# Latent cross-attention of a two-layer decoder: the context's keys and values between the first projections, the second batch's rows among the first batch's scores

## The chip, the core and the metric

The kernel runs as one program on one core of a Trainium2 chip. The metric is the device time of one execution in microseconds. The engines are named as the profile names them: PE does the matmuls and the transposes (PEld is its weight load), DVE, ACT and POOL do elementwise work and reductions, SP issues the DMAs. Each engine works through its own queue in order; an instruction waits for the semaphores of the engines whose results it needs.

## What is computed

The program is a decoder of two layers on `x` of shape 4 x 1024 x 256 (four batches, 1024 rows, 256 features), float32, with a context of 4 x 77 x 256. Layer 0 is causal attention, cross-attention and a quantised feed-forward; layer 1 is an attention with a convolution over the heads, the latent cross-attention, and a mixture of experts. The change touches the latent cross-attention and what is prepared for it inside the layer-1 attention. Its reference, cut to what matters (`x` is the context here, `latents` are the normalised rows of the decoder):

```python
xn = layernorm(x, ln_x_g, ln_x_b)            # 77 context rows of a batch
ln = layernorm(latents, ln_l_g, ln_l_b)      # 1024 rows of a batch
q = ln @ W_q
kv = concat([xn @ W_kv, ln @ W_kv], axis=1)  # 77 + 1024 keys and values
k, v = kv[..., :256], kv[..., 256:]          # then 4 heads of 64
qn = rmsnorm(q, q_gamma) * 64 ** -0.5
kn = rmsnorm(k, k_gamma)
sim = where(full_mask, qn @ kn.T, neg)       # the mask hides context rows only
out = softmax(sim) @ v @ W_out + b_out       # added to x of the decoder
```

## The kernel before, in words

**The stage.** `Latents.run` (L1874) does the latent cross-attention, batch after batch. Its PSUM has two rotating slots named `pt` for projections and transposes (`ps_t`, `bufs=2`), one set of score tiles, one of outputs. A tile of a name takes the next slot of that name and waits until the one before in that slot has been read. The order of PE, ACT and DVE is the order in which the Python code records the instructions (`manual_schedule`), so generators that are advanced by `next` decide what stands between what.

**The pieces of the work.**
- `of_context` (L1911) makes the context's keys and values. For each of the four batches it projects 77 rows (L1919, two matmuls 512 wide), copies the keys out and squares them on ACT (L1922, L1924), copies the values on DVE (L1925) and sums the squares (L1926). Then come the inverse root mean squares of all four (L1900 and the steps L86 to L94), the scaling of the keys (L1907), and for each batch two transposes (L1935) whose results two DVE instructions copy into `kcT` with the factor gamma (L1938). In the kernel before this runs as one block, and its keys stand in a tile `k`.
- `projected(b)` (L1942) does the same for the 1024 rows of a batch, in eight tiles of 128 rows: key and value projection (L1956), query projection (L1958), four ACT instructions (L1960, L1961, L1963, L1964), the value copy on DVE (L1962) and the sum of squares (L1965). Then the inverse roots (L1900, L86 to L94, L1976), scaling of the keys in two halves (L1907) and transposes of queries and keys in groups of four (L1983) which ACT copies out (L1984). It yields after each tile, and five times in the rest: 13 steps.
- `rows(b)` (L1815) normalises the rows of a batch of `x`: statistics in two halves on DVE (L1823, L1824), inverse roots (L101, L86 to L94), normalisation in two halves of four DVE instructions (L118), and for each half two groups of four transposes (L1838) that two ACT instructions each copy out (L1811).
- `ahead(b, got)` (L2122) advances `projected(b)` and, from its tenth step on, `rows(b + 1)`: 16 steps.
- The unit: for a batch, for four pairs of row blocks, two head pairs and two blocks there are 16 units. In each, the scores are computed on PE (L2008, L2012, L2016), their maxima on DVE (L2021, L2023, L2024), exponentials on ACT (L2035, L2041), the probabilities of the unit before are transposed (L2058, L2065) and copied (L2059, L2066), and the values are weighed (L2090). Each unit advances the next batch's preparation, `coming = ahead(b + 1, got)`, by one step.
- `add_row` (L156) adds the output's bias to a whole batch of `x` on POOL. `projected(b)` calls it after its first tile, and it waits until `rows(b)` has read `x`.

**The order at the start of the stage.** The small constants are prepared (L2136 to L2147), then `of_context()` runs as a block, then all 16 steps of `ahead(0)`, that is the projections of batch 0 with the rows of batch 1 in the last steps, and only then the first unit.

**What runs earlier.** The layer-1 attention `l1_attn` takes a generator `beside` (defined in `network`) that it advances once in four scores, 16 times in the last batch, and to the end when its own work is over. It yields from `latents.context` (normalises and transposes the context, L1864) and `latents.rows(0)`. There `pt` has a single slot. In `rows` of the kernel before, the two groups of transposes of a half stand in one step; the second group needs the slot of the first. The attention's own chain per score is PE L1520, DVE L1528, POOL L1530, DVE L1538, ACT L1541, and PE weighs the values of four scores together (L1549).

## Time and profile before

| what | value |
|---|---|
| median of 3 runs | 4223.02 us (4222.13 to 4224.56) |
| the profiled execution, own time | 4222.46 us |
| its span | 4220.7 us |
| PE busy | 3950.9 us, 94% of the span |
| DVE busy | 2984.2 us, 71% |
| ACT busy | 1622.8 us, 38% |
| POOL busy | 1019.4 us, 24% |
| mean granted clock of PE | 0.973 |
| first context projection (L1919) starts | 2892.03 us |
| first projection of batch 0 (L1956) starts | 2911.48 us |
| first scores (L2008) of batch 0, 1, 2, 3 start | 2956.86, 3118.65, 3293.51, 3462.52 us |

The profile tells the times of one execution, counted from the start of its span. A timeline row gives start, duration, engine, line, what is written from what, and behind it the idle time ahead of it with the engine that ended it. PE's clock can be granted in full or in part; the profile gives its mean for a stretch.

### The profile page before, as it was taken

The page shows a single profiled execution, that of the slowest core. Times are in us where ns is not written, and L with a number is a line of the kernel's source. Part 1 is how long each engine was busy: PE and PEld are TensorE (multiplying, and loading weights), DVE is VectorE, ACT ScalarE, POOL GpSimd, SP SyncE. Part 2 cuts the span into 40 slices and gives each one's busy share as a digit, 9 for nine tenths or more (in the row PEclk, how much of TensorE's full clock was granted, in tenths as well). Part 3 has the DMA queues.
Part 4 walks back from the last instruction along what each step waited for, and adds up shares of the span by engine and source line. Part 5 has one row for each costly group of instructions (what it writes and reads, how often), then busy time and mean ns, then how long its engine had stood idle before and what let it go on. Part 6 is the DMA issues. An engine that isn't in the chain of part 4 may idle for free.

```text
span 4220.7 us, 58215 instructions
## 1 busy us (share of the span) xinstructions
PE 3950.9 (94%) x22392; PEld 2841.7 (67%) x22392; DVE 2984.2 (71%) x5514; ACT 1622.8 (38%) x2601; POOL 1019.4 (24%) x1218
## 2 busy tenths in 40 slices
PE   8899568999999999999999999997989899899999
PEld 6644335887788887888878877784555555557765
DVE  6646688888878888788878889776566567543324
ACT  4334355334333343333433333332555454212221
POOL 1100000433333433334333343331000000012215
PEclk9989889999999999999999999998999999899999
DMA  2010000000000000000000000000000000302213
GB/s 68 2 40 1 1 23 1 1 1 1 1 1 1 1 1 1 1 1 1 1 1 1 1 1 1 1 1 27 1 1 1 1 1 11 114 23 62 63 43 109
DMA packets 50911, 64.37 MB, mean 15 GB/s; under 512 B 8557, under 2 KB 44769, under 8 KB 50625
## 3 DMA queue, kind: packets, MB, share of 16 engines
q1 hardware_dynamic: 44145, 42.81, 3.2%
q0 software_dynamic: 6480, 17.70, 1.5%
q8 instruction: 185, 3.03, 0.3%
q14 instruction: 101, 0.83, 0.1%
HBM read 42.80 MB, written 17.69 MB: 14 GB/s over the span
## 4 chain that ended last, share of the span: by engine, by line
PE 67%; DVE 15%; ACT 1%; issue 1%; DMA 0%; SPq 0%; DVEq 0%; ACTq 0%
PE sc L1520 35%; PE po L1549 5%; PE ph L2572 4%; PE ph L2500 3%; PE sc L2008 3%; DVE mx L1528 3%; DVE pr L1538 3%; DVE nm L2021 3%; PE po L2090 2%; PE po L2602 2%; PE po L2487 2%; PE pt L1956 2%; DVE prT L2059 1%; DVE km L1510 1%; PE pt L2058 1%
## 5 line engine op out<-in xcount | busy, mean ns | idle before, releaser
L1520 PE MATMUL sc<-qT,km 128*128 128x256 f32 x8064 | 1793.1, 381 | 8.8 <-DVE pr L1538 8.8
L1520 PEld LDWEIGHTS sc<-qT,km 128*128 128x128 f32 x8064 | 1521.4, 190 | 273.7 <-issue 61.4
L1541 ACT ACTIVATE pr<-pr,zb 128x1024 f32<-128x1024 f32 x512 | 588.2, 1149 | 1326.3 <-DVE pr L1538 1298.5
L1530 POOL PARTITION_ALL_REDUCE top<-mx x512 | 544.6, 1064 | 1465.6 <-DVE mx L1528 1465.6
L1528 DVE TENSOR_REDUCE mx<-sc 128x256 f32<-128x1024 f32 x512 | 625.4, 1221 | 321.3 <-PE sc L1520 320.0
L1538 DVE TENSOR_TENSOR pr<-sc,top 128x1024 f32<-128x1024 f32 x512 | 621.0, 1213 | 0.0
L1510 DVE SCALAR_TENSOR_TENSOR km<-kT,w_L_attn_conv_w,km 128x512 f32<-128x512 f32 x504 | 380.3, 757 | 25.2 <-ACT km L1497 20.4
L1533 POOL COPY tops<-top 32x256 f32<-32x256 f32 x512 | 269.9, 527 | 32.6
L1549 PE MATMUL po<-pr,v 128*32 128x256 f32 x4096 | 248.4, 383 | 0.0
L2021 DVE TENSOR_REDUCE nm<-sc 128x1 f32<-128x1024 f32 x128 | 156.1, 1220 | 77.3 <-PE sc L2008 77.2
L2035 ACT ACTIVATE pr<-sc,nb,rq 128x1024 f32<-128x1024 f32 x128 | 155.0, 1211 | 128.0 <-PE pt L2065 110.6
L1549 PEld LDWEIGHTS po<-pr,v 128*32 128x32 f32 x4096 | 120.3, 110 | 109.3 <-issue 42.7
L2572 PE MATMUL ph<-wgu,xnT 128*128 x568 | 179.8, 459 | 0.6 <-ACT xnT L2561 0.6
L1497 ACT ACTIVATE km<-kT,w_L_attn_conv_w 128x512 f32<-128x512 f32 x252 | 173.5, 706 | 5.3 <-PE po L1303 5.3
L2579 DVE TENSOR_TENSOR xnT<-ph,xnT 128x352 f32<-128x352 f32 x71 | 37.2, 524 | 187.7 <-ACT xnT L2578 187.7
L2058 PE MATMUL pt<-ident,pr 128*128 128x128 f32 x1024 | 142.9, 280 | 22.2 <-DVE X L2109 12.8
L2073 POOL COPY rb<-rinv 128x256 f32<-128x256 f32 x32 | 12.8, 400 | 591.4 <-DVE rinv L2049 313.9
L2058 PEld LDWEIGHTS pt<-ident,pr 128*128 128x128 f32 x1024 | 111.6, 142 | 47.3 <-issue 18.8
L2090 PE MATMUL po<-prT,v 128*64 128x256 f32 x1024 | 133.5, 393 | 0.2 <-DVE oT L2097 0.2
L2572 PEld LDWEIGHTS ph<-wgu,xnT 128*128 128x128 f32 x568 | 102.3, 190 | 46.0 <-ACT xnT L2561 0.9
L2008 PE MATMUL sc<-kT,qT 64*128 64x512 f32 x512 | 130.8, 615 | 0.3 <-ACT pr L2035 0.3
L2059 ACT COPY prT<-pt 128x512 f32<-128x512 f32 x128 | 68.9, 588 | 142.3 <-PE pt L2058 142.3
(518 smaller groups left out, 4882.6 us busy)
## 6 DMA issues: line engine op xcount, KB each, us to landing
yrows<-xnT SPq DMA_DIRECT2D x71, 128.0 KB, 1.7
X<-in_x SPq DMA_DIRECT2D x8, 512.0 KB, 7.3
out<-X SPq DMA_DIRECT2D x8, 512.0 KB, 3.1
wgu<-in_L_ffn_w_gate SPq DMA_DIRECT2D x8, 352.0 KB, 6.4
wgu<-in_L_ffn_w_up SPq DMA_DIRECT2D x8, 352.0 KB
raw<-in_L_ffn_w1T SPq DMA_DIRECT2D x4, 512.0 KB, 3.5
raw<-in_L_ffn_w2T SPq DMA_DIRECT2D x4, 512.0 KB, 3.6
xrows<-xn SPq DMA_DIRECT2D x2, 1024.0 KB, 4.5
```

Of the source, the lines that this page charges most:

```text
L1510: nc.vector.scalar_tensor_tensor(km, keys, weight, km, ALU.mult, ALU.add)
L1520: nc.tensor.matmul(sc[:, j, :], km[:, c, bass.ts(j, P)], qT[:, c, bass.ts(i, Q2)], start=(c == 0), stop=(c == 1),)
L1528: nc.vector.tensor_reduce(mx, sc.rearrange("p j q -> p q j"), AX.X, ALU.max)
L1530: nc.gpsimd.partition_all_reduce(top, mx, P, bass_isa.ReduceOp.max)
L1533: nc.gpsimd.tensor_copy(tops[n][rows, i % (NQ, 2)[n], :], top[rows])
L1538: nc.vector.tensor_tensor(pr, sc, top.unsqueeze(1).to_broadcast([P, KT, Q2]), ALU.subtract)
L1541: nc.scalar.activation(pr, pr, AF.Exp, bias=zb[:, h : h + 1])
L1549: nc.tensor.matmul(po[32 * e : 32 * e + 32, :], v[:, n * KT + j, 4 * g + e, :], prs[e][:, j, :], start=(j == 0), stop=(j == KT - 1),)
L2008: nc.tensor.matmul(sc[e][:, bass.ts(n, 512)], lhsT[at], kT[at, d, bass.ts(n, 512)], start=True, stop=True,)
L2021: nc.vector.tensor_reduce(nm, sc[e], AX.X, ALU.max, negate=True)
L2058: nc.tensor.transpose(pt[:, n, :], pr[e][:, bass.ts(j + n, P)], net.ident)
L2572: nc.tensor.matmul(ph[:, k, :F], s["xT"][:, c, :], wgu[:, bass.ds(s["e"] * GU + (2 * c + k) * F, F)], start=(c == 0), stop=(c == 1),)
```

## The change

The change has three parts. No arithmetic is added or left out.

1. `of_context` becomes a generator of ten steps; its keys stand in a buffer of `v` instead of `k`, and the copy with gamma into `kcT` goes from DVE to ACT. At the start of the stage four of its steps alternate with the first four tiles of `projected(0)`; the small constants come after these, and the rest of the context stands between the later steps of `projected(0)`.
2. `rows(1)` is no longer done ahead of the first scores. `ahead(1)` does it first, in three steps, within the first three units of batch 0, and squeezes `projected(1)` and `rows(2)` into the other 13.
3. `rows(0)`, beside the layer-1 attention, gets `fine=True`: a yield after each group of four transposes.

```diff
-    def rows(self, b, ps):
+    def rows(self, b, ps, fine=False):
...
                     self.lg, self.lb,
                 )
+                if fine:
+                    yield
...
             def of_context():
-                kc = p1.tile([P, NTB, D], F32, name="k")[:Z, :B]
+                kc = p2.tile([P, NTB, D], F32, name="v")[:Z, :B]
...
                         sums[:, b, :], sq.rearrange("p (h d) -> p h d", h=H), AX.X, ALU.add
                     )
+                    yield
                 flat = sums.rearrange("p b h -> p (b h)")
                 r = inverse_rms(flat, Z, B * H, "rc").rearrange("p (b h) -> p b h", h=H)
+                yield
                 times_rms(kc, r, Z)
+                yield
...
-                        nc.vector.tensor_scalar(
-                            kcT[at, :, b, e, :], pt[at, :2, :Z], gk[at], None, ALU.mult
+                        nc.scalar.activation(
+                            kcT[at, :, b, e, :], pt[at, :2, :Z], AF.Copy, scale=gk[at]
                         )
+                    yield
...
             def ahead(b, got):
+                if b == 1:
+                    for k, _ in enumerate(self.rows(b, ps_t)):
+                        if k % 2:
+                            yield
+                    yield
                 now, rows = projected(b, got), self.rows(b + 1, ps_t) if b + 1 < B else iter(())
-                for k in range(16):
+                for k in range(16 if b > 1 else 13):
                     next(now, None)
-                    if k >= NTB + 1:
+                    if b == 1 and k == 12:
+                        next(now, None)
+                    for _ in range((k >= NTB + 1) + (b == 1 and k > 10)):
                         next(rows, None)
                     yield
...
+                kcT = w.tile([P, 2, B, 2, Z], F32, name="kcT")
+                nc.gpsimd.memset(kcT, 0.0)
+                vc = w.tile([P, B, D], F32, name="vc")
+                got = []
+                now, context = projected(0, got), of_context()
+                for _ in range(4):
+                    next(context)
+                    next(now)
                 nc.vector.tensor_scalar(gq, gq, float(dh) ** -0.5, None, ALU.mult)
...
-                of_context()
-                got = []
-                for _ in ahead(0, got):
+                for k in range(12):
+                    next(now, None)
+                    if k in (0, 2, 5, 6, 7, 8):
+                        next(context, None)
+                for _ in chain(context, now):
                     pass
...
-                        yield from latents.rows(0, ps)
+                        yield from latents.rows(0, ps, fine=True)
```

More of the change, by code (lines that the diff above doesn't have):

```diff
@@ L2144, in run @@
                 nc.vector.memset(first[0:1], 1.0)
-                kcT = w.tile([P, 2, B, 2, Z], F32, name="kcT")
-                nc.gpsimd.memset(kcT, 0.0)
-                vc = w.tile([P, B, D], F32, name="vc")
-                of_context()
-                got = []
-                for _ in ahead(0, got):
+                for k in range(12):
[3 more added lines that the diff above has]
+                for _ in chain(context, now):
                     pass
```

## The prediction

> **What bounds the kernel now.** I read first the busy time by stretches of the latent stage (length, then busy time and instructions of PE, PEld, DVE, ACT, POOL, then PE's granted clock, DMA share, GB/s), with a second cut for the clock:

> ```profile
> 2892.00:2911.50 19.50, 9.07 (x25) 3.38 (x25) 12.45 (x34) 2.69 (x8) 5.33 (x2) 0.85 0.48 146
> 2911.50:2940.00 28.50, 25.96 (x72) 13.25 (x72) 9.57 (x19) 11.01 (x33) 0.00 (x0) 0.92 0.00 1
> 2940.00:2957.00 17.00, 9.13 (x42) 7.08 (x44) 13.71 (x53) 7.61 (x14) 2.07 (x1) 0.60 0.00 0
> 2957.00:3118.70 161.70, 146.25 (x854) 85.57 (x854) 106.49 (x243) 88.60 (x208) 9.77 (x9) 0.98 0.00 1
> ```
> ```profile
> 2943.00:2957.00 14.00, 7.89 (x34) 6.24 (x36) 11.09 (x40) 5.55 (x10) 2.07 (x1) 0.51 0.00 0
> 2957.00:2962.00 5.00, 5.00 (x20) 2.36 (x20) 3.02 (x5) 2.35 (x5) 2.45 (x1) 1.00 0.00 0
> ```

> The context's block (row 1) and the stretch between the last projection and the first scores (row 3) are bound by DVE's chain, with PE half idle; the projections (row 2) and batch 0's units (row 4) fill PE. Then the timeline names the waits:

> ```profile
> 2900.20 4.48 POOL L156 TENSOR_TENSOR X<-X,r_L_xattn_b_out 128x2048 f32<-128x2048 f32 x1 [7.35 <-issue]
> ...
> 2901.66 3.05 DVE L1900 TENSOR_SCALAR ss_c<-ss_c 77x16 f32<-77x16 f32 x1
> ...
> 2908.37 0.75 PE L1935 MATMUL pt<-ident,k 77*128 77x77 f32 x4 [8.21 <-DVE k L1907]
> ...
> 2918.30 1.03 PE L1958 MATMUL pt<-w_L_xattn_W_q,xnT 128*128 128x256 f32 x4
> ...
> 2919.68 1.98 PE L1956 MATMUL pt<-w_L_xattn_W_kv,xnT 128*128 128x512 f32 x4 [0.34 <-DVE v L1962]
> ...
> 2952.73 1.98 PE L1838 MATMUL pt<-ident,xn 128*128 128x128 f32 x8 [3.14 <-DVE xn L118]
> ```

> PE stands 8.21 us for the context's roots, and 3.14 us for batch 1's normalisation, which the first scores do not need. In the layer-1 attention the same view shows PE waiting for ACT at the second group of four transposes of `rows(0)`, twice:

> ```profile
> 2637.23 1.12 PE L1838 MATMUL pt<-ident,xn 128*128 128x128 f32 x4 [4.29 <-ACT xnT L1811]
> ...
> 2660.26 1.11 PE L1838 MATMUL pt<-ident,xn 128*128 128x128 f32 x4 [3.44 <-ACT xnT L1811]
> ```

> **Part 1: context between the projections.** A tile runs from key projection to key projection in 3.20 us (2916.48 to 2919.68): 1.82 until PE starts the query (2918.30), then ACT's two readings, DVE's value copy and the slot. A context projection has the same four records as the key projection, so 1.82 more per piece, if the slots allow. They do: the query's slot is freed by the context's value copy, which ends about 3.14 after the piece's start (2.03 to ACT's first reading as from 2916.48 to 2918.51, 0.66 for both, 0.45 for DVE), and PE wants it at 3.64. Four pieces: 4 x 5.02 = 20.1 us. Wq's DMA starts at 2891.66 and lands in 2.7 us, ahead of the first use at 2895.7.

> Then four tiles, 4 x 3.20 = 12.8. DVE must do beside them the constants (0.15, 0.32, 0.31, 0.11, 0.17: 1.06), the context's roots (2.45: rows 2904.75 to 2907.01 and 0.20 for L1900 unblocked, as at 2939.93) and the scaling (1.22). Between its sum and the next value copy it is idle 1.64; the constants and the scaling fit, the roots are late by 0.8. From the last tile's end to its sum's end 1.1 (2938.83 to 2939.90). Sum: the last sum is ready 20.1 + 12.8 + 0.8 + 1.1 = 34.8 after the first context matmul; before, 2939.90 - 2892.03 = 47.9. POOL's addition, which held L1900 for 3.05 us, meets only value copies and sums there, and L1925 and L1926 ran at 0.42 and 0.40 inside it. If the constants and the scaling found no idle DVE, they would add 2.3. No DMA is moved, and POOL keeps its order here: the zeroing of `kcT`, then the addition. The keys' new buffer is one of the two of `v`: batch 1's values take it long after its last reading, and batch 2's wait for batch 0's last weighing, as now (DVE idles 11.61 us before L1962 at 3137.52).

> **Part 2a: rows(1) taken from ahead of the scores.** From that sum to the first scores now: 2956.86 - 2939.90 = 17.0. After: 4.5 to the first key transposes, unchanged (2944.41). DVE's second scaling follows the first at once, without the four statistics pairs between (2.05). Then two rounds of eight key transposes with two context groups between and behind, by ACT's copies: four at 0.69 and four of the `kcT` form. That form is not shown on ACT; the copy of 77 x 256 starts its successor 0.26 later, L2059's 512 columns take 0.59; I take 0.37, DVE's present time. With transposes at half clock (1.94 per eight, as now) the scores start 9.7 after the sum, at full clock 8.4; I take 9.1. First scores at 34.8 + 9.1 = 43.9, before 64.8: **-20.9 us**.

> **Part 2b: rows(1) in the first three units.** Batch 0 takes 161.8 us now (first scores 2956.86 to 3118.65). Starts of the scores give the costs: units without preparation, from the last batch, 8.60, 9.50, 7.75, 8.22; units with a tile, from unit 3 of batch 0, 10.84, 11.38, 12.08, 10.52.
> - Units 0 to 2: now 28.2. Unit 0's maxima end at 4.9; eight statistics pairs (4.24) push the next maximum to 9.2, where it is at 9.03 now, as a tile's copy and sum stood there. In unit 1, roots (2.4) and half the normalisation (1.36) follow DVE's last copy at 13.9: next maximum 17.8, now 20.05, as the tile at half clock (3.62) is gone. In unit 2 come 16 transposes through two slots, each group waiting for two ACT copies (0.96) behind unit 2's exponentials: scores 3 at 27.0. Gain 1.2, with no tile done.
> - Units 3 to 10: eight tiles, 55.7 as now for the first five and 34.0 for three that have other work now: 89.6.
> - Unit 11 roots 8.3. Units 12, 13 query transposes with half the statistics each, 9.8 and 10.7 (now 10.67, 9.25 on other base units). Unit 14 key transposes with roots and normalisation: DVE 9.9, I take 10.0. Unit 15 key transposes (1.0) and all 16 row transposes: four waits for 0.96 us of ACT behind the exponentials, 8.2 + 1.0 + 4.0 = 13.2.
> Sum 27.0 + 89.6 + 8.3 + 9.8 + 10.7 + 10.0 + 13.2 = 168.6 against 161.8: **+6.8 us**.

> POOL's addition for batch 1 moves from 2954.93 to the end of unit 2's normalisation. Queued behind it are the copies `rb`, needed two units on. It can stop DVE:

> ```profile
> 3099.39 4.53 POOL L156 TENSOR_TENSOR X<-X,r_L_xattn_b_out 128x2048 f32<-128x2048 f32 x1 [15.10 <-DVE xn L118]
> ...
> 3102.16 1.78 DVE L2024 SCALAR_TENSOR_TENSOR nb<-nm,nx,rq 128x1 f32<-128x1 f32 x1
> ```

> L2024 takes 0.22 elsewhere and here ends when POOL does: 1.56 lost. In unit 2 POOL would run from 24.3 to 28.8 and the next L2024 stand at 30.5, so I count nothing; the bounds are 0 and 1.56. [...]

> **Part 3: four transposes at a time.** From one weighing of values (L1549) to the next takes 15.88 us where nothing stands beside. With the first normalisation it took 18.35 (2612.07 to 2630.42), with group, wait, group and second normalisation 23.89, with group, wait, group 21.77: 8.01 + 5.89 = 13.90 extra. After: four intervals with one group each and one with the normalisation (2.47). A group costs between 0.26 (the four context transposes at 2533.7: 16.14) and its own 1.12 at half clock; I take 0.6: 2.47 + 4 x 0.6 = 4.9. **-9.0 us**, between -11 and -7. The cover is the slot: its copies must be done 14 us later, where 4.29 was enough now.

> **Sum.** -20.9 + 6.8 - 9.0 = -23.1, so 4222.46 - 23.1 = 4199.4 for the profiled execution. The median of the runs lies 0.56 above it: **4200.0 us**.

> **Rivals.**
> - *Half clock in the first units* (0.16). With the tiles gone from units 0 to 2, PE idles for DVE and ACT; now 2943 to 2957 stood at 0.51, and the clock rose just when the scores began. If all three units' scores (2.7 each on the path, with sx and mask) run at half clock: 3 x 2.7 = 8.1, 4208.1. For it: the idle times in units 0 and 1; against: scores follow densely packed projections. [...]
> - *The rows come due in batch 0* (0.12): rows(2), squeezed into units 14 and 15, makes DVE and ACT the bound and adds its DVE time again (statistics apart: 2.4 + 2.7 + 1.2) and 4 more of waits: +10.3, 4210.3.
> - *fine changes nothing* (0.08): the group waits for a slot at another place, since there is only one. Without part 3: 4209.0.
> - *Slower* (0.03): PE's half clock lasts through the tile units of batch 0. A unit has some 10.5 us of PE work, so each unit at half clock adds up to that; 2.2 such units eat the 23.1 us, and with four the time is 4199.4 + 0.6 + 42 = 4242. Against it: in batch 0 the clock is 0.98, as tiles and scores keep PE filled.

> **How the numbers follow.** The forecast has 0.61. Its own bounds: part 1 and 2a +-2, 2b +-4, part 3 +-2, so 4193 to 4207. The range reaches up to the rivals at 4208 to 4210 and leaves some 0.13 out: 4193 to 4211. Differences within 0.2% (8.4 us, about what a measurement of this kernel can tell from none) need 14.7 us of the gain lost: two rivals together, 0.04 of their 0.36. Faster 0.93, slower 0.03.

> **What would show it.** First scores 44 us after the first context matmul; the pieces every 5.0 us; no L1900 of 3 us; intervals of L1549 with single groups near 16.5; batch 0 near 168.6 between first scores. The forecast is wrong if a piece takes 6 or more (a slot wait I missed), if the clock row of the first 20 us of batch 0 is near 0.5, or if unit 15 takes over 17.

## The result, and the profile after

The changed kernel takes **4195.34 us** (median of 4 runs, 4194.45 to 4199.97), the kernel before on the same chip 4222.58 us (4 runs, 4219.43 to 4224.56): ratio 0.9941, 95% interval 0.9925 to 0.9956 (the quotient of the two medians, 0.9935, lies inside it). A later comparison (run e9 below) gave 0.9941 again (0.9927 to 0.9954). The prediction was 4200.0 us, range 4193 to 4211, faster with 0.93: the direction is right, the range holds the time, and the forecast is 4.7 us too slow.

The profiled execution has a span of 4192.5 us, before 4220.7. Here is where the 28.2 us between them lie, from the starts of the groups of records in both traces (line numbers of the changed kernel, where the scores are L2014, the context projections L1921):

| stretch | before, us | after, us | difference | predicted |
|---|---|---|---|---|
| start to the weighing of values (L1549) at 2496.33 / 2488.91 | 2496.33 | 2488.91 | -7.4 | 0 |
| from there to the last L1549 (`rows(0)` beside) | 386.86 | 374.63 | **-12.2** | -9.0 |
| from there to the first context matmul | 8.84 | 8.81 | 0.0 | 0 |
| first context matmul to first scores | 64.83 | 43.28 | **-21.6** | -20.9 |
| batch 0, first scores to first scores | 161.79 | 171.91 | **+10.1** | +6.8 |
| batches 1, 2 and 3 | 474.62 | 475.89 | +1.3 | 0 |
| last scores to the end | 627.41 | 629.07 | +1.7 | 0 |

The first row has nothing to do with the change: no instruction differs there. The same weighing stands at 2490.91, 2493.92, 2498.69, 2497.40, 2495.68, 2492.03 and 2491.14 in the profiled executions of e1 to e6 and e9, whose instructions up to there are all the same. What differs is PE's clock: up to 2488 us it was granted in half for 112.6 us in this execution and for 136.5 us in the one of before, and over the fourteen profiled executions the weighing tends to start later the longer that time is (from 2488.91 us with 112.6 to 2498.92 us with 146.8, in e7). So one pair of profiles can be up to 10 us apart before the edit begins, and the change itself is worth -20.8 us by the rows behind the first.

The windows that answer to the ones of before (length, then busy time and instructions of PE, PEld, DVE, ACT, POOL, then PE's granted clock, DMA share, GB/s); the rows are the projections with the context, the way from the last sum to the first scores, units 0 to 2, and the rest of batch 0:

```profile
2872.00:2906.00 34.00, 30.49 (x88) 14.71 (x88) 15.98 (x44) 13.46 (x41) 5.63 (x2) 1.00 0.29 84
2906.00:2915.60 9.60, 6.79 (x33) 4.95 (x32) 5.15 (x17) 6.69 (x14) 0.00 (x0) 0.69 0.00 0
2915.60:2946.60 31.00, 24.93 (x97) 12.89 (x96) 21.34 (x62) 15.81 (x37) 4.04 (x2) 0.76 0.00 1
2946.60:3087.50 140.90, 128.89 (x774) 76.20 (x772) 92.35 (x218) 76.17 (x179) 7.06 (x8) 1.00 0.00 1
```

The block of 19.5 us with PE half idle is gone: context and projections are one stretch of 34 us, 90% PE, at full clock. The poor stretches are now the second and the third, at a clock of 0.69 and 0.76. The timeline of PE shows both (start, duration, engine, line, out<-in, count, idle time ahead and what ended it):

```profile
2872.35 1.94 PE L1921 MATMUL pt<-w_L_xattn_W_kv,cT 128*77 128x512 f32 x4 [0.52 <-DVE X L1608]
2874.13 1.88 PE L1962 MATMUL pt<-w_L_xattn_W_kv,xnT 128*128 128x512 f32 x4
2875.85 1.03 PE L1964 MATMUL pt<-w_L_xattn_W_q,xnT 128*128 128x256 f32 x4
2877.22 1.94 PE L1921 MATMUL pt<-w_L_xattn_W_kv,cT 128*77 128x512 f32 x4 [0.34 <-DVE v L1968]
...
2908.43 0.35 PE L1940 MATMUL pt<-ident,v 77*128 77x77 f32 x2
2910.57 1.94 PE L1989 MATMUL pt<-ident,k 128*128 128x128 f32 x8 [1.79 <-DVE k L1909]
...
2915.63 3.79 PE L2014 MATMUL sc<-kT,qT 64*128 64x512 f32 x8
2919.35 0.81 PE L2018 MATMUL sx<-kcT,qT 128*128 128x154 f32 x2
2920.00 0.23 PE L2022 MATMUL sx<-mrow,first 128*128 128x77 bf16 x2
2922.60 5.17 PE L2014 MATMUL sc<-kT,qT 64*128 64x512 f32 x8 [2.36 <-ACT pr L2041]
...
2946.65 1.99 PE L2014 MATMUL sc<-kT,qT 64*128 64x512 f32 x8
```

A piece (L1921 to the next L1921) takes 4.87 us and its projections wait only 0.34 for a slot. Eight score matmuls take 1.99 us in unit 3; in unit 0 they take 3.79 and in unit 1 5.17, which includes a wait for ACT inside the group.

In the attention, the waits of 4.29 and 3.44 us ahead of the second group are gone: a weighing of values (L1549), then one group of 0.66 us, no wait, and the next weighing 16.27 us after the last.

```profile
2623.03 1.93 PE L1549 MATMUL po<-pr,v 128*32 128x256 f32 x32
2624.89 0.66 PE L1838 MATMUL pt<-ident,xn 128*128 128x128 f32 x4
...
2639.30 1.93 PE L1549 MATMUL po<-pr,v 128*32 128x256 f32 x32
2641.16 0.66 PE L1838 MATMUL pt<-ident,xn 128*128 128x128 f32 x4
...
2655.56 1.93 PE L1549 MATMUL po<-pr,v 128*32 128x256 f32 x32
...
2671.52 1.93 PE L1549 MATMUL po<-pr,v 128*32 128x256 f32 x32
```

### The profile page after: what moved, and what is told of

Read it like the earlier page. It is cut to its first block, busy times and chain, and to the rows that moved or that the text cites. A ratio compares the mean times of both kernels' runs of the same rounds, so it can differ in the third digit from the quotient of the medians.

```text
span 4192.5 us, 58206 instructions
## 1 busy us (share of the span) xinstructions
PE 3941.7 (94%) x22392; PEld 2833.7 (68%) x22392; DVE 2978.4 (71%) x5506; ACT 1626.6 (39%) x2609; POOL 1019.4 (24%) x1218
## 4 chain that ended last, share of the span: by engine, by line
PE 68%; DVE 15%; ACT 1%; issue 1%; DVEq 0%; ACTq 0%
PE sc L1520 35%; PE po L1549 5%; PE ph L2594 4%; PE ph L2522 3%; PE sc L2014 3%; DVE mx L1528 3%; DVE nm L2027 3%; DVE pr L1538 3%; PE po L2096 2%; PE po L2624 2%; PE po L2509 2%; PE pt L1962 1%; DVE prT L2065 1%; DVE km L1510 1%; PE pt L2064 1%
## 5 line engine op out<-in xcount | busy, mean ns | idle before, releaser
L1528 DVE TENSOR_REDUCE mx<-sc 128x256 f32<-128x1024 f32 x512 | 625.7, 1222 | 308.5 <-PE sc L1520 307.3
L1549 PE MATMUL po<-pr,v 128*32 128x256 f32 x4096 | 248.4, 383 | 0.0
L1549 PEld LDWEIGHTS po<-pr,v 128*32 128x32 f32 x4096 | 120.2, 110 | 109.3 <-issue 42.7
L2079 POOL COPY rb<-rinv 128x256 f32<-128x256 f32 x32 | 12.8, 400 | 632.0 <-DVE rinv L2055 389.9
L2014 PE MATMUL sc<-kT,qT 64*128 64x512 f32 x512 | 136.0, 629 | 2.6 <-ACT pr L2041 2.4
```

Source lines behind the costliest of these rows:

```text
L1528: nc.vector.tensor_reduce(mx, sc.rearrange("p j q -> p q j"), AX.X, ALU.max)
L1549: nc.tensor.matmul(po[32 * e : 32 * e + 32, :], v[:, n * KT + j, 4 * g + e, :], prs[e][:, j, :], start=(j == 0), stop=(j == KT - 1),)
L2014: nc.tensor.matmul(sc[e][:, bass.ts(n, 512)], lhsT[at], kT[at, d, bass.ts(n, 512)], start=True, stop=True,)
```

## The experiments

All runs are compared with runs of the kernel before on the same chip; e1 to e4 shared one chip, e5 to e8 a second, e9 to e11 a third, and e12 ran on a fourth. Since the total moves by several us without an edit, most verdicts below rest on the intervals of the trace. "Front" is first context matmul to first scores; "batch 0" is first scores of batch 0 to first scores of batch 1, and so on.

| run | time, us | ratio (95%) | front | units 0-2 | batch 0 | batch 1 | batch 2 |
|---|---|---|---|---|---|---|---|
| before, profiled | 4222.46 | | 64.8 | 28.2 | 161.8 | 174.9 | 169.0 |
| after, profiled | 4194.45 | | 43.3 | 31.0 | 171.9 | 175.6 | 169.5 |
| e1 part 3 alone | 4206.66 | 0.9968 (0.9956-0.9980) | 65.1 | 28.4 | 161.9 | 175.3 | 169.1 |
| e2 part 1 alone | 4204.21 | 0.9960 (0.9947-0.9974) | 50.75 | 28.4 | 162.0 | 175.0 | 169.0 |
| e3 part 2 alone | 4217.58 | 0.9992 (0.9983-1.0001) | 56.3 | 28.5 | 169.4 | 175.4 | 169.2 |
| e4 added matmuls | 4192.05 | 0.9927 (0.9912-0.9942) | 41.9 | 26.8 | 167.6 | 172.4 | 169.4 |
| e5 parts 1 and 3 | 4201.69 | 0.9949 (0.9936-0.9963) | 50.75 | 29.0 | 160.9 | 172.9 | 169.5 |
| e6 later tiles | 4196.98 | 0.9937 (0.9922-0.9952) | 43.1 | 29.8 | 170.7 | 169.6 | 165.3 |
| e7 e4 and e6 | 4192.36 | 0.9926 (0.9912-0.9939) | 41.9 | 26.8 | 167.6 | 170.3 | 165.3 |
| e8 shifted normalisation | 4201.59, one run | | 42.7 | 29.9 | 170.8 | 175.4 | 169.2 |
| e9 changed kernel again | 4195.36 | 0.9941 (0.9927-0.9954) | 43.1 | 29.9 | 170.75 | 175.0 | 169.3 |
| e10 e4 and e8 | 4191.20 | 0.9926 (0.9913-0.9940) | 41.9 | 26.8 | 167.65 | 172.4 | 169.2 |
| e11 e4, e6 and e8 | 4186.93 | 0.9917 (0.9903-0.9930) | 41.9 | 26.8 | 167.65 | 170.4 | 165.1 |
| e12 added transposes | 4198.62, one run | | 41.9 | 28.7 | 169.6 | 173.0 | 169.7 |

**e1: part 3 alone.** The kernel before with `fine`:

```diff
-                        yield from latents.rows(0, ps)
+                        yield from latents.rows(0, ps, fine=True)
```

> The kernel before with the single transpose groups of rows(0) alone (part 3). Theory: the part stands by itself. From the first weighing of values (L1547 or so, as the lines stand) behind rows(0)'s start to the last one, the extra over 15.88 us a piece falls from 13.90 to about 1.6 us, as in the changed kernel: 12.2 us, so 4210.4 against 4222.6, and all behind it in the latent stage as before (front 64.8 us from the first context matmul to the first scores, batch 0 161.8 us). Rival (drift): the 12.2 us were partly a luck of the clock windows in one profiled execution; then the extra is 5 us or so here, as predicted (-9.0), and the time is 4213 to 4214. A step of the clock windows ahead of the attention, where the instructions are the same, may move the profiled times by several us either way: that the 7.4 us by which the changed kernel was early there are of this kind is shown if this kernel's own first weighings stand elsewhere too.

Measured: from the same weighing to the last one 374.61 us, before 386.86: -12.25, and 13.5 by the ratio (0.0032 x 4222). The part stands by itself and everything behind is as before. The rival falls.

**e2: part 1 alone.** The changed kernel's start of the stage, with the old `ahead`, with `rows(0)` as before (no `fine`), and with

```diff
+                rows = self.rows(1, ps_t)
                 for k in range(12):
                     next(now, None)
                     if k in (0, 2, 5, 6, 7, 8):
                         next(context, None)
+                    if k > 4:
+                        next(rows, None)
-                for _ in chain(context, now):
+                for _ in chain(context, now, rows):
```

> The context's keys and values between the first batch's projections (part 1), with rows(1) left ahead of the first scores and rows(0) as before. Theory: the last sum is ready 33.7 us after the first context matmul (before 47.9, changed kernel 33.7): -14.2; from there to the first scores 17.0 as before plus some 1.5 for the keys' transposes that now stand there: first scores at 52.2 instead of 64.8, -12.6; batch 0 161.8 as before. Time 4222.6 - 12.6 = 4210. Rival: the interleaving hides nothing by itself, since DVE's chain of statistics, roots and rows(1) sets the first scores and just waits longer: first scores at 60 or later, time 4218 or more; then the front's gain in the changed kernel came from the moved rows.

Measured: last sum 33.70 us after the first context matmul, first scores at 50.75, so -14.1, and 17.05 between them where 17.0 stood before. The keys' four groups of transposes added nothing: they fit into the waits of that stretch, where PE still stands for DVE.

```profile
2929.41 1.94 PE L1989 MATMUL pt<-ident,k 128*128 128x128 f32 x8 [1.79 <-DVE k L1909]
2931.27 0.52 PE L1940 MATMUL pt<-ident,v 77*128 77x77 f32 x2
2932.65 1.94 PE L1989 MATMUL pt<-ident,k 128*128 128x128 f32 x8 [0.86 <-DVE k L1909]
2934.52 0.52 PE L1940 MATMUL pt<-ident,v 77*128 77x77 f32 x2
2937.73 1.99 PE L1838 MATMUL pt<-ident,xn 128*128 128x128 f32 x8 [2.69 <-DVE xn L118]
```

The rival (no gain of its own) falls. The time fell by 16.9 (0.0040 x 4222), more than the 14.1 of the stretch; its first weighing was 2.4 us earlier.

**e3: part 2 alone.** The new `ahead` in the kernel before, with `projected(0)` run to its end behind the context's block:

```diff
-                for _ in ahead(0, got):
+                for _ in projected(0, got):
                     pass
```

> rows(1) among batch 0's first units and rows(2) squeezed into its last (part 2 alone); the context as a block ahead, rows(0) as before. Theory: the front loses 17.0 - 8.5 = 8.5 us (first scores at about 56.3 after the first context matmul), and batch 0 costs 10 us more, as in the changed kernel (units 0 to 2 at 31 of 28.2, the last five at 51 against about 44): sum +1 to +2 us, 4224 against 4222.6, no difference that a measurement tells. Rival (the sum on record): batch 0 costs 6.8 and the front gives more, since rows(1) was 6.7 of it: -2 to -4 us, 4219 to 4221. Second rival: the half clock in units 0 to 2 of the changed kernel came from the front's interleaving; then units 0 to 2 take 27 here.

Measured: front 56.3 (-8.5), batch 0 169.4 (+7.6): -0.9 in the stage, ratio 0.9992 with 1 inside its interval. Taken by themselves the moved rows pay back what they gain. Units 0 to 2 take 28.5, between the two theories, at a clock of 0.85 against 0.76 in the changed kernel's first profile:

```profile
2950.70:2979.20 28.50, 21.91 (x97) 11.68 (x96) 21.27 (x62) 15.35 (x35) 2.90 (x2) 0.85 0.00 1
```

**e4: matmuls that nothing reads, where PE waits.** The changed kernel with a `filler(pool, name, n, times)` that writes `times` matmuls of 128 x n into a free tile:

```diff
                     if k in (0, 2, 5, 6, 7, 8):
                         next(context, None)
+                    if k == 6:
+                        filler(ps_o, "po", 256, 4)
...
                                 sc, sx, nb = scores(b, batch, d, i + u)
+                                if b + i + d + u == 0:
+                                    filler(ps_t, "pt", 512, 2)
```

> The changed kernel with matmuls added that nothing reads: four of 128x256 ahead of the key transposes (where PE waits 1.79 us for the scaled keys) and two of 128x512 between the first and the second unit's scores (where it waits 2.36 us). They add about 4 us of PE work where PE waited. Theory (half clock): they keep PE's clock up; the key transposes take 1.1 instead of 1.95 us per eight, the scores of units 0 and 1 2.0 instead of 3.8 and 5.2, and from the last sum to the first scores it is 8.2 instead of 9.6, units 0 to 2 take 27 to 28 instead of 31.0: 4 us less in all. Rival (DVE and ACT bound these units, and the long scores are only waits in PE's rows): the clock rises in the profile or not, but units 0 to 2 stay at 31, or become longer by what the added matmuls take (33). The total, 4191 or 4195 to 4197, is near the limit of what the rounds tell; the intervals between the scores decide.

Measured: 8.2 us from the last sum to the first scores (9.6 without), units 0 to 2 in 26.8 (31.0), so 5.6 us less than in the first profile of the changed kernel (4.2 less than in e9), although PE does 3.9 us more work. The timeline (L2120 is the added work) shows the rest:

```profile
2919.60 1.94 PE L2120 MATMUL po<-w_L_xattn_W_kv 128*128 128x256 f32 x8
2921.55 1.06 PE L1989 MATMUL pt<-ident,k 128*128 128x128 f32 x8
...
2925.26 1.99 PE L2014 MATMUL sc<-kT,qT 64*128 64x512 f32 x8
...
2927.61 1.96 PE L2120 MATMUL pt<-w_L_xattn_W_kv 128*128 128x512 f32 x4
2930.42 1.12 PE L2014 MATMUL sc<-kT,qT 64*128 64x512 f32 x2 [0.86 <-ACT pr L2041]
2931.81 1.98 PE L2014 MATMUL sc<-kT,qT 64*128 64x512 f32 x6 [0.27 <-ACT pr L2041]
```
```profile
2917.00:2925.20 8.20, 6.81 (x41) 4.70 (x40) 5.13 (x17) 6.53 (x14) 0.00 (x0) 1.00 0.00 0
2925.20:2952.00 26.80, 21.14 (x102) 11.22 (x100) 21.00 (x62) 15.71 (x37) 3.11 (x2) 0.94 0.00 1
```

The same eight key transposes take 1.06 instead of 1.94, the same scores 1.99 instead of 3.79, and the clock of the stretches is 1.00 and 0.94. The half clock is shown as the cause, and the rival falls. e7, e10 and e11 give the same 8.2 and 26.8 each, and e6, e8 and e9, without the added work, 9.0 to 9.4 and 29.8 to 29.9.

**e5: parts 1 and 3 without the moved rows**, e2 with the line of e1.

> The two parts of e1 and e2 together, with rows(1) left ahead of the first scores and no rows moved. Theory (the parts add up): extra of rows(0) 1.6 us (-12.3), first scores 50.8 us after the first context matmul (-14.1), batch 0 at 162: -26.4, so 4195.5 against 4222, the same as the changed kernel, whose moved rows gained 7.5 in front and cost 10.1 in batch 0. Rival (the front's gain needs the moved rows, or the parts share a gain): 4201 or more.

Measured: in the stages the parts add up (374.62 us of attention, front 50.75, batch 0 160.9: -27.2 in all). The time is 0.9949, 21.5 us less, 6 short of it, and the trace has that behind the latents: 635.2 us from the last scores to the end (before 627.4, e4 629.1). Against e4, whose instructions there are the same, it is 6.1 us more: 3.2 us are six expert blocks that each take 0.4 to 0.6 us longer, as they do in e6, e7 and e8 on this chip; 1.6 us come at the start of the mixture of experts, in steps of 0.4 us from matmul to matmul, where half-clock windows lie; and 1.3 us come near the end, where PE stands idle at full clock. By the total, e5 stands behind the changed kernel, but the two intervals overlap; which is better is left open. In the stage alone (front and batch 0 together) e5 takes 211.7 us and e2 212.7, the changed kernel 215.2 in the first profile and 213.8 in e9, and e4 209.5: there the moved rows cost 1 to 3.5 us more than they gain, and gain 2 to 3 only together with the added matmuls of e4. The same matmuls without the moved rows were not tried.

**e6: the tiles of batches 2 and 3 one unit later.** Both kernels have a wait of DVE at the start of batches 1 and 2, for the value buffer (profile of before):

```profile
3137.52 0.42 DVE L1962 COPY v<-pt 128x256 f32<-128x256 f32 x1 [11.61 <-PE po L2090]
```

```diff
                 for k in range(16 if b > 1 else 13):
-                    next(now, None)
+                    if b == 1 or k:
+                        next(now, None)
```

> The changed kernel with the preparation of batches 2 and 3 started one unit later (their first projected tile stands in unit 1 of the batch before, not in unit 0, all that follows in projected() one unit later; rows() stays). Theory: the wait of DVE for the value buffer at units 0 and 1 of batches 1 and 2 (11.6 us before the first value copy, some 8 of it on the path) is there because the copy stands in DVE's order ahead of the weighing that frees the buffer. Started one unit later it is gone: unit 0 at 8.6, unit 1 at about 12 (before 11.4 and 20.2): 8 us less in each of the two batches, 4179 against 4195. Rival: the wait only moves into the next unit, or comes back at the end of the batch, where the key transposes now stand beside the row transposes: 4190 or more.

Measured: units 0 and 1 of batch 1 take 8.61 and 12.08 (before the edit 11.39 and 20.16), but units 8, 10 and 13 got longer (by 2.8, 4.8 and 1.5 us; unit 10 from 9.26 to 14.04), and units 9 and 14 shorter (by 1.2 and 3.0). The batches fall by 6.0 and 4.2 us, not 8 each. Part of the 6.0 is the clock: batch 1 stood 3.4 us at half clock here and 10.2 in the first profile. Between e4 and e7, which have 10.2 us of it each in the two batches together, the same edit is worth 2.0 and 4.1 us. The time did not move (0.9937 against 0.9941), since from the last scores to the end it took 637.5 us where the first profile has 629.1; 3.0 of these 8.4 us are the six expert blocks of e5, and 2.2 are one wait of PE near the end. What the rival said is partly true. In the step of unit 9 the roots (3.1 us of DVE) and four statistics pairs (2.1) now stand together, where the roots stood alone in the step of unit 8, and the wait for them falls into unit 10. In e11, which has the same edit, PE waits 4.06 us for DVE there, and the clock is half behind that wait (0.50 from 3206 to 3210):

```profile
3206.39 1.12 PE L2066 MATMUL pt<-ident,pr 128*128 128x128 f32 x4 [4.06 <-DVE X L2117]
```

**e7: e4 and e6 together.**

> e6 with the added matmuls of e4. Theory: the half clock of the first units and the wait for the value buffer are two costs at different places, so the gains add: 8 us twice from the tiles, 5.7 from the clock (first scores 41.9 us after the first context matmul, units 0 to 2 at 26.8), 4174 to 4176. Rival: with PE packed less at batches 1 and 2, the clock falls to half there, and gives back what the wait took: 4182 or more.

Measured: batches 1 and 2 6.2 us shorter than in e4 together, and the same time as e4 (0.9926): behind the last scores it took 635.3 us where e4 took 629.1. The total expected was 16 to 18 us too low: 10 of it because the two batches gained 6 on e4 and not 16, the rest on the far side of the stage. The time is one that the rival allows (4182 or more), but its reason does not hold in sum: the clock stood at half for 10.2 us in batches 1 and 2 together, as long as in e4.

**e8: the first normalisation one weighing later.**

```diff
         for h in range(2):
             ts = slice(h * NTB // 2, (h + 1) * NTB // 2)
+            if fine and h == 0:
+                yield
             net.normalize(y[:, ts], x[:, ts], mv[:, ts], r[:, ts])
```

> The changed kernel with one empty piece ahead of the first normalisation in rows(0), so that it and all groups behind it stand one weighing later in the layer-1 attention. Theory: the 2.48 us of the interval in which the first normalisation stands are not its price as such; DVE has 2.4 us of joining two heads' outputs in that interval already, and the 1.3 us of normalisation come on top of an engine that is full. One interval on, DVE idles about 0.44 us ahead of each maximum: the interval with the normalisation is 15.9 to 16.0 there, as with the second one, and the interval it leaves falls from 18.36 to about 17.1: 1.2 us less. Rival: the normalisation costs 2.5 wherever its first half stands (it waits for the buffer of the rows, or its reads collide): 18.3 moves on by one interval, and the one it left is 15.88.

Measured: the interval it left falls from 18.36 to 17.06, as the theory says; the one it went to is 16.81, 0.93 over the base, where I expected 0.1. So 2.48 was 1.18 of joining plus 1.30 of normalisation, and the normalisation's price is what DVE lacks in slack: 1.30 beside the joining, 0.93 just behind it, where DVE is still late, 0.07 three intervals on, 0.00 for the second half here. The shift gains 0.4 us in these intervals, not 1.2. In DVE's rows of e8, L1528 follows without a gap behind the normalisation, and the usual gap of 0.44 ahead of it comes back two to three maxima later (0.36, then 0.44):

```profile
2634.87 1.38 DVE L118 TENSOR_SCALAR xn<-X,mv,ri_y 128x256 f32<-128x256 f32 x4
2636.16 1.22 DVE L1528 TENSOR_REDUCE mx<-sc 128x256 f32<-128x1024 f32 x1
...
2639.09 1.22 DVE L1528 TENSOR_REDUCE mx<-sc 128x256 f32<-128x1024 f32 x1
...
2642.46 1.23 DVE L1528 TENSOR_REDUCE mx<-sc 128x256 f32<-128x1024 f32 x1 [0.36 <-PE sc L1520]
...
2645.91 1.22 DVE L1528 TENSOR_REDUCE mx<-sc 128x256 f32<-128x1024 f32 x1 [0.44 <-PE sc L1520]
```

**e9, e10, e11: the changed kernel and two better ones on one chip.** e10 has the edits of e4 and e8, e11 that of e6 as well.

> The changed kernel itself, beside the next two kernels on one chip. Its intervals in the stages that the change touches should come out as in the first profile: 33.7 us from the first context matmul to the last sum, 9.0 to 9.6 from there to the first scores, units 0 to 2 of batch 0 near 30 to 31, single groups in the attention 16.27. What falls elsewhere (the first weighing of values near 2489 there, near 2496 in the kernel before) differs from run to run by several us. The time is 4193 to 4198.

> The changed kernel with the added matmuls of e4 and the empty piece of e8. Theory: -5.7 from the clock of the first units and -1.2 from the normalisation add up to 7 us below the changed kernel of this call: 4187 to 4190, units 0 to 2 at 26.8. Rival: half-clock windows elsewhere take it back: less than 3 us below.

> As e10, and batches 2 and 3 prepared one unit later, as e6. Theory: e6's batches 1 and 2 were 10 us shorter between their first scores (169.6 and 165.3 instead of 175.6 and 169.5), and what e6 lost behind them (637.5 us from the last scores to the end instead of 629.1) belonged to that chip and its clock windows, since e5, which shares none of the edit, lost 6 of it as well: 15 to 17 us below the changed kernel of this call. Rival: the shift brings the end of the latent stage into another position against the clock windows each time, and the loss behind it stays: 7 to 10 us below, no better than e10.

Measured: 4195.36, 4191.20 and 4186.93 us. The changed kernel repeats its intervals. e10 is 4.2 below it (7 expected, less than 3 by the rival), e11 8.4 below (15 to 17 expected, 7 to 10 by its rival). In the stages both did what e4 and e6 did. In the profiles, from the weighing at 2491 to 2496 us to the end, e10 lies 8.9 us below e9 and e11 12.8. Ahead of it, where all three run the same instructions, they are 2.2 and 4.5 us later, and this takes back part of the gain there. From the last scores to the end e11 took 629.7 us, about as long as e9 (629.0), so what e6 lost behind its scores did not come with the edit. e11 has the lowest median, 0.9917 (0.9903 to 0.9930) of before, and is clearly faster than that kernel; its interval overlaps with that of the changed kernel by 0.0003, so that it beats the changed kernel too is likely but only just not shown.

**e12: transposes in place of the added matmuls**, 15 at each of the two places (the body of `filler`; what it writes is not read here either):

```diff
-                for _ in range(times):
-                    nc.tensor.matmul(t, wkv[:, 0, :P], wkv[:, 0, :n], start=True, stop=True)
+                for k in range(15):
+                    nc.tensor.transpose(t[:, :P], wkv[:, 0, bass.ts(k % 4, P)], net.ident)
```

> e4 with other added work at the same two places and of the same length: 15 transposes of 128x128 each (some 2 us at full clock) in place of matmuls. Theory: it is matmuls that hold the clock, transposes do not; the key transposes and the first scores run at half clock again, 9.0 us or more from the last sum to the first scores and 30 or more for units 0 to 2, plus what the transposes take beyond the waits they stand in. Rival: any work that keeps PE from idling holds it: 8.2 and 26.8, as in e4.

Measured: 8.21 us to the first scores, as in e4, and units 0 to 2 in 28.7, between the two. At the first place transposes held the clock as well as matmuls; PE had nothing but transposes from 2912.98 to 2922.26, 9.3 us, and the clock stayed at 1.00 there:

```profile
2912.70:2922.20 9.50, 7.70 (x55) 5.74 (x55) 6.00 (x18) 7.49 (x16) 0.00 (x0) 1.00 0.00 0
```
```profile
2916.62 1.80 PE L2120 MATMUL po<-ident,w_L_xattn_W_kv 128*128 128x128 f32 x15
2918.56 1.06 PE L1989 MATMUL pt<-ident,k 128*128 128x128 f32 x8
...
2922.26 1.99 PE L2014 MATMUL sc<-kT,qT 64*128 64x512 f32 x8
...
2924.61 1.83 PE L2120 MATMUL pt<-ident,w_L_xattn_W_kv 128*128 128x128 f32 x15
2927.43 1.12 PE L2014 MATMUL sc<-kT,qT 64*128 64x512 f32 x2 [0.98 <-ACT pr L2041]
2928.82 3.60 PE L2014 MATMUL sc<-kT,qT 64*128 64x512 f32 x6 [0.27 <-ACT pr L2041]
```

At the second place the scores behind them still fell to half (3.60 for six against 1.98 in e4). The theory, that transposes do not hold the clock, falls at the first place: what the changed kernel lacks there is work on PE, of either kind. At the second place the half clock comes in windows of 3.41 us (see the last section), and they lay alike in both executions: one begins 0.08 us behind the start of the first scores in e4 and 0.05 us ahead of it in e12. In the window that holds the wait ahead of the six scores PE was busy for 2.29 us with matmuls alone in e4, and for 2.16 us, 0.82 of them transposes, in e12. Whether the transposes or the 0.13 us less of work made the difference is left open.

## Why the prediction was right, step by step

- **Part 1, the pieces** (5.02 us each): 4.87. The last sum was forecast for 34.8 us after the first context matmul and came at 33.7; the roots made the tiles late by 0.40 (3.59 instead of 3.19 us at 2895.01), not 0.8. That POOL's addition would hold no L1902 was right.
- **Part 2a, sum to scores** (9.1): 9.57 in the first profile, 9.35 in e9, 8.2 at full clock in e4, where 8.4 was worked out. `kcT` on ACT, which no row of before had shown, took 0.37 in the estimate and 0.37 to 0.39 in fact (0.77 for two).
- **Part 2b, units 0 to 2** (27.0): 31.0 in the first profile, 29.9 in e9. This term failed, by the rival "half clock in the first units" (0.16), which priced all three units' scores at half clock, +8.1; it came to 4.2 in the first profile against the 26.8 of e4. The DVE and ACT working behind 27.0 fits: e4 shows 26.8, with one half-clock window left in it. I had the idle times of PE in front of me and argued them away with "scores follow densely packed projections"; between the projections and the scores stand transposes and a wait of 1.79 us.
- **Units 3 to 10** (89.6): 89.65. **Units 11 to 15** (52.0): 51.24. That `rows(2)` comes due was priced rightly, and POOL's addition (4.53 us from 2942.96) held no DVE instruction, which was the 0 I took.
- **Part 3** (-9.0): -12.2. Right mechanism, wrong sizes: a single group cost 0.39, not 0.6, and the second normalisation 0.07, not 2.47. I read the 2.47 off the first normalisation's interval and took all of it as its price; e8 shows half of it is joining work of that interval, and the rest depends on DVE's slack.
- **Batches 1 to 3 and the end** (0): +3.0 in the first profile. Of it 1.7 is one half-clock window, in the mixture of experts, and e3 and e10 lack it; the rest lies at the start of batches 1 and 2.

Of the signs of being wrong that the prediction named, none came: a piece took 4.87 us, unit 15 took 13.1, and the clock of the first 20 us of batch 0 was 0.72. The sign for the clock was set near 0.5, though, so the half clock that did come in units 0 to 2 passed under it.

The errors are +3.3 in batch 0 and +3.0 behind it against -3.2 in the attention and -0.7 in front, so the sum is close (-20.8 without the first row against -23.1) partly because they offset each other. That they offset each other is luck. In e9, where units 0 to 2 took 29.9 us instead of 31.0, the same rows give -22.1. The ratio says -24.9 (0.0059 x 4222; its interval, -18.6 to -31.7, holds all three) and the medians -27.2, so the 4.7 us between forecast and median are not more than the measurement's own uncertainty.

## What to carry to other kernels

An interval that is long is not the price of the one thing you see in it: compare it with the same work beside another engine load before you take its length as a cost. Moving work from a bound stretch into the next one gains only if the next one has slack on the engine the work needs (in e3 the front gained 8.5 us and batch 0 lost 7.6), and PE's waits have a second price there: the clock of the matmuls behind a wait can fall to half (behind the 2.36 us ahead of unit 1's scores in the changed kernel it was 0.50 from 2924 to 2930), and added matmuls that nothing reads can be worth it when they stand in those waits (4 to 6 us gained here in the stage). With gains of 0.3%, read the intervals around the edit: totals moved by 8 us between executions of the same instructions.

## What the runs showed of the hardware

In the changed kernel a window with 2.02 us of transposes, 1.40 of waits and no matmul (2906.31 to 2909.73) was followed by half clock (0.50 in the next). In the kernel before, one with 2.23 us of work, all but 0.02 of it transposes, and 1.19 of waits (2977.22 to 2980.64) was followed by full clock, and e12's stretch of transposes alone, 7.70 us of work in 9.50, stayed at 1.00. The length of the waits alone does not tell: a window of the changed kernel with 1.85 us of matmuls and 1.56 of waits (2868.77 to 2872.18) had full clock behind it.

Nor did transposes alone keep the clock at half: in the kernel before, a window at half clock with 3.15 us of them and no matmul (2953.33 to 2956.74) had full clock behind it. What decides between half and full clock these runs do not settle.
